# Three scatter accumulators in place of four, and a last round of ten grouped quads, in a message-passing layer on one Trainium2 core

## The chip, the cores and the metric

The kernel runs on one core of a Trainium2 chip. The core has five engines with a queue of instructions each, which run in order: TensorE (PE) multiplies matrices, VectorE (DVE) works on whole tiles, ScalarE (ACT) evaluates functions and copies, GpSimd (POOL) here mostly issues scatters, and SyncE (SP) issues loads and stores. Engines wait for one another by semaphores. The metric is the time of one execution on the device, in microseconds (us).

## The reference

The layer has 6250 nodes with 128 features and 200,000 edges. Each edge has a source node `src`, which receives, a node `dst`, from which it takes features, 20 attributes and a weight. The edges are sorted by `dst`; `src` is random.

```
h   = relu(layernorm(x)) @ W_in                       # 6250 x 128
W   = (softplus(f @ W_f1 + b_f1) - log 2) @ W_f2 + b_f2   # 200000 x 128
m   = h[dst] * W * weight                             # 200000 x 128
agg = segment_sum(m, src)                             # 6250 x 128
out = x + (softplus(agg @ W_o1 + b_o1) - log 2) @ W_o2 + b_o2
```

## The kernel before, in words

Edges are taken in chunks of 128, one to a partition: 1563 chunks, or 391 **quads** of four chunks (512 edges). One loop runs over items 0 to 398; each item does a stage of several neighbouring quads, so that all engines have work: the filter of quad i+1 (`s1_pe`, `s1_exp`, `s1_ln`), gather and product of quad i-1 (`s2_pe_x`, `s2_pe_w`, `s2_copy`, `s2_m`, lines 505 to 536), the last stages of quads i-2 to i-4. The order within an item is written out by hand at the loop's end (lines 1225 ff.). Everything else is hung into it by `at(item, point, function)`: points L (loads on SP), D0 to D2, DM and DR (DVE), A0 to A2 (ACT), PE1 and PE2 (PE), and S, the end of the item, for scatters. The kernel is scheduled by hand; each engine takes its instructions in that order.

`dst` is sorted, so a quad gathers from a short window of rows by a one-hot product. `src` is random, so the sum over edges is the hard part. A quad is summed in one of three ways:

- **plain** quads (31 of them: the first 12, and 19 at the end). `s3_pe` adds up rows of the same node within a chunk by a product with an equality matrix, `s3_copy` moves the result into a tile `s` (four buffers), `s3_ji` makes the indices `ji`, and `s3_scatter` adds 128 rows of 512 bytes to an accumulator in DRAM, one scatter a chunk, in item q+4.
- **listed** quads (192). The product is written into `s` at once and scattered in item q+2. Rows of a node that stands twice in a chunk go to a list area behind the accumulator. Windows of 16 listed quads each get their list ready ahead (`l_eq` to `l_take`) and are finished by `l_load`, which reads the list rows of every accumulator, `l_sum`, which adds them, and one more scatter.
- **grouped** quads (168; from quad 8 on, at steps of 2, 2, 2 and 3). `rank_group` and what follows it (lines 603 to 672) work out, for eight quads at a time, a slot for each edge by its node's group; `perm_oh` and `permute` move the rows to their slots (four blocks of 128) by one-hot products, `perm_out` copies them into `mst`. After a **round** of eight grouped quads four **units** follow (`unit_oh`, `unit_pe`, `unit_evac`): each adds one block of all the round's quads into `accT`, a transposed accumulator in SBUF. The units of the last round stand at items 389, 391, 393 and 395. Rows that find no slot are gathered for two quads at a time (`over_pe` to `over_int`) and scattered once (`over_scatter`, tiles `os` and `oji`).

All scatters are indirect DMAs that POOL issues from line 597, in the order of the program. `acc_of` gives the accumulator by the running count of scatters: accumulator 0 alone for the first two, two in turn up to the eighth, three in turn up to the 140th, four in turn up to the 923rd (`RET`, all but the last 64), and then accumulators 1 to 3. Two scatters to one accumulator don't overlap: the later one waits until the earlier one has landed. The accumulators are cleared by DMAs (`zero_piece`, line 168, and `zero_list`, line 173) during the first items.

As nothing goes to accumulator 0 after the 923rd scatter, items 376 to 397 read it early: `r0_load` (line 1084), four transposes in `r0_tp` (line 1091) and an addition to `accT` in `r0_add` (line 1097), for each of 13 groups of 512 nodes.

Behind the loop a few flags are worked out on DVE (lines 1285 to 1290); all engines read them, and there is a repair path that doesn't run with these inputs. Then the **tail** reads accumulators 1, 2 and 3 (`t_load`, line 1378), adds them up, transposes, adds `accT` and computes the output layer, for 13 groups of nodes. `over_int` (line 769) makes the scatter's indices on ACT in the item after the sum, at its end (point A2), from what DVE made in the same item.

Of the kernel before, what the change touches and what calls it, by code (L numbers as in the profile page):

```python
# [7 lines left out]
F32 = mybir.dt.float32  # L8
# [12 lines left out]
P = 128  # L21
# [5 lines left out]
SLOTS = GRP * CAP + OVC  # L27
MP0 = 8
MPGAPS = (2, 2, 2, 3)
MPEND = 0  # L30
RND = 8
EXTRA = 0
RKQ = 8
UOFF = (2, 6)
SW = 16
# [8 lines left out]
WSEG = 256  # L44
HB = 64
NR = 3 * WIN
NACC = 4
FPARTS = ((0, 3), (3, 2), (5, 1))
CQ = 16
EARLY_N = 256  # L50
# [4 lines left out]
def tile_gnn(ctx: ExitStack, tc: tile.TileContext, x, fB, cT, srcT, srcr, dstr, win_, wf1, wf2, bias, bo1c, wo1,  # L55
# [20 lines left out]
    GN = NP // GRP  # L76
    ZR = 10 if ACC_R % 10 == 0 else 1
    ZL = 3
    K1_END, K2_END, K3_END = 2, 8, 140
    Z2, Z3 = [0,0,1,1,2,2,3,3,4,4], [5+2*j for j in range(10)]  # L80
    mpq = sorted_quads(NQ)
    mpi = {q: n for n, q in enumerate(mpq)}
    units = unit_its(mpq)
# [4 lines left out]
    CE = min(128, EP // P) if spread else EP // P  # L88
    CB = min(4 * NS + 64, EP // P) if spread else 0
    lend = splain[LE - 1] if LE else 0  # L90
    scat = [0] * (NQ + 60)
    for q in splain:
        scat[q + (2 if LB <= plain[q] < LE else 4)] += min(4, NCH - 4 * q)
    NW = (LE - LB) // SW
    LR = P * NW
    wend = [splain[LB + SW * (w + 1) - 1] for w in range(NW)]
    for w in range(NW):
        scat[wend[w] + 16] += 1
    for q in mpq[1::2] + mpq[-1:] * (len(mpq) % 2):
        scat[q + 10] += 1  # L100
    RET = max(120, sum(scat) - 64)
    ret_at = min(i for i in range(len(scat)) if sum(scat[:i + 1]) >= RET)

    cp = ctx.enter_context(tc.tile_pool(name="cp", bufs=1))
    dp = ctx.enter_context(tc.tile_pool(name="dp", bufs=1, space=DRAM))
# [475 lines left out]
    def acc_of(k):  # L581
        if k < K1_END:
            return 0
        if k < K2_END:
            return k % 2
        if k < K3_END:
            return k % 3
        if k < RET:
            return k % 4
        return 1 + k % 3  # L590

    sc_n = [0]

# [9 lines left out]
    def rank_group(r):  # L603
        qs = mpq[RKQ * r:RKQ * r + RKQ]
        nc4 = 4 * len(qs)
        srcf = wk.tile([P, 4 * RKQ], F32, tag="srcf", name="srcf", bufs=1)
        o = 4 * (NS + RKQ * r)
        nc.vector.tensor_copy(srcf[:, :nc4], srcT_sb[:, o:o + nc4])
        srcf = srcf[:, :nc4]
        n = [P, nc4, GRP - 1]  # L610
        nc.vector.tensor_tensor(ge[:, :nc4, 1:GRP], srcf.unsqueeze(2).to_broadcast(n),
                                thr.unsqueeze(1).to_broadcast(n), op=ALU.is_ge)
        G = wk.tile([P, 4 * RKQ, GRP], BF16, tag="G", name="G", bufs=1)
        nc.vector.tensor_tensor(G[:, :nc4], ge[:, :nc4, :GRP], ge[:, :nc4, 1:], op=ALU.subtract)
        cnt = wk.tile([P, 4 * RKQ], F32, tag="cnt", name="cnt", bufs=1)
        nc.vector.tensor_reduce(cnt[:, :nc4], ge[:, :nc4, 1:GRP], axis=AX.X, op=ALU.add)
        loc = wk.tile([P, 4 * RKQ], F32, tag="loc", name="loc", bufs=1)
        nc.vector.scalar_tensor_tensor(loc[:, :nc4], cnt[:, :nc4], float(-GN), srcf, op0=ALU.mult, op1=ALU.add)
        ext = wk.tile([P, 4 * RKQ, 3], BF16, tag="ext", name="ext")
        nc.vector.memset(ext[:, :, 0], 0.0)  # L620
        nc.vector.tensor_scalar(ext[:, :nc4, 1], loc[:, :nc4], float(-(GN // 2)), None, op0=ALU.add)
        nc.vector.tensor_copy(ext[:, :nc4, 2], cnt[:, :nc4])
        rk[r] = {"G": G[:, :nc4], "cnt": cnt[:, :nc4], "ext": ext, "n": nc4, "qs": qs}

    def before_me(ps_t, src, w):
        n = src.shape[1]
# [223 lines left out]
    with tc.manual_schedule():  # L850
# [145 lines left out]
            at(2 * k + 3 if spread else 0, "D2", half_piece, k)  # L996
        for j in range(ZR):
            at(Z2[j] if spread else 0, "L", zero_piece, nc.sync, 2, j)
        for j in range(ZR):
            at(Z3[j] if spread else 0, "L", zero_piece, nc.sync, 3, j)  # L1000
        for g in range(1, NG):
            if not spread:
                xt_load(g)
# [74 lines left out]
        def large_all():  # L1078
            nc.vector.tensor_scalar(zcol[:, 3:4], late["lps"][:, 0:1], 0.0, None, op0=ALU.is_gt)

        def r0_load(g):
            o, T = tgroups[g]
            t_ = ld.tile([P, 4, P], F32, tag="fb", name="r0t", bufs=2)
            nc.sync.dma_start(wide(t_[:, :T], T), rows(accs[0], o, T))
            pst["r", g] = t_

        def r0_tp(g):
            T = tgroups[g][1]
            tp = ps.tile([P, 4, P], F32, tag="B", name="rtp", bufs=4)
            for t in range(T):  # L1090
                nc.tensor.transpose(tp[:, t, :], pst["r", g][:, t, :], idt)
            pst["p", g] = tp

        def r0_add(g):
            o, T = tgroups[g]
            v = nodes(accT, o, T)
            nc.vector.tensor_tensor(v, tiles(pst["p", g], T), v, op=ALU.add)

        def x_bias(t):
            n = min(4, NPT - t)  # L1100
            v = x_sb[:, t:t + n]
# [20 lines left out]
        for t in range(0, NPT, 4):  # L1122
            i = mid + 8 * (t // 4) if spread else 0
            at(min(i + 9, NQ + 1), "D2", x_bias, t)
        r0_at = 0
        for g in range(len(tgroups)):
            i = clear(max(r0_at + 1, ret_at + 5), units)
            r0_at = i
            at(i - 2, "L", r0_load, g)
            at(i, "PE2", r0_tp, g)  # L1130
            at(i + 1, "D0", r0_add, g)
        for r in range(-(-len(mpq) // RKQ)):
            i = mpq[RKQ * r]
            i = max(i, 6)
            at(i - 6, "D2", rank_group, r)
            at(i - 5, "PE2", rank_count, r)
            at(i - 4, "D0", rank_own, r)
            k = mpq[RKQ * r] if i == 6 else i - 2
            at(k, "PE2", rank_over, r)
            at(k + 1, "D0", rank_slot, r)  # L1140
# [3 lines left out]
        for w in range((LE - LB) // SW):  # L1144
            for g in range(4):
                n = LB + SW * (w - 1) + 4 * g
                i = splain[n] + 2 if w else 6 + 2 * g
                while w and (i - MP0) % sum(MPGAPS) not in UOFF:
                    i -= 1
                for k in range(2):  # L1150
                    kk = (LB + SW * w + 4 * g) // 2 + k
                    at(max(0, i + k - 2), "L", sb_load, kk)
                    at(i + k, "DM", l_eq, kk)
                i = clear(i + 2, units)
                at(i, "PE2", l_count, (LB + SW * w) // 4 + g)
                at(i + 1, "D0", l_dup, w, g)
            i += 1
            at(i, "D0", l_scan, w)
            i = clear(i, units)
            at(i, "PE2", l_before, w)  # L1160
            at(i + 1, "D0", l_index, w)
            assert i + 1 <= splain[LB + SW * w] + 1
            at(i + 2, "D2", l_id, w)
            i = clear(i + 3, units)
            at(i, "PE2", l_place, w)
            at(i + 1, "D0", l_take, w)
            i = clear(wend[w] + 12, units)
            at(i, "L", l_start, w)
            at(i, "A0", l_dg, w)
            at(i, "PE2", over_row, ("L", w))  # L1170
            at(i + 1, "D0", l_same, w)
            k = clear(i + 1, units)
            at(k - 1, "L", l_load, w)
            at(k, "PE2", l_sum, w)
            at(k + 1, "A0", l_copy, w)
            at(k + 1, "DM", l_ji, w)
            at(k + 1, "A2", over_int, ("L", w))
            at(k + 2, "S", over_scatter, ("L", w))
        if LE:
            for k in range(NACC):  # L1180
                for j in range(ZL):
                    at((0, 3, 6, 9)[k] + j + 1, "L", zero_list, k, j)
        for q in mpq:
            at(q + 1, "D2", perm_oh, q)
            at(q + 2, "DR", part_rem, q, 1)
# [11 lines left out]
            if mpi[q] % 2 or q == mpq[-1]:  # L1197
# [9 lines left out]
                at(k, "PE2", over_sum, q)  # L1207
                at(k + 1, "A0", over_copy, q)
                at(k + 1, "DM", over_ji, q)
                at(k + 1, "A2", over_int, q)  # L1210
                at(k + 2, "S", over_scatter, q)
        last = mpq[-1]
        for r in range(len(mpq) // RND):
            for s, k in enumerate(unit_slots(mpq, r)):
# [2 lines left out]
                at(k, "PE2", unit_pe, r, s)  # L1217
                at(k + 1, "D1", unit_evac, r, s)

        banked = (prep_tp, prep_mm, rank_count, rank_over, permute, over_pe, over_row, over_sum, late_bias, r0_tp,  # L1220
                  l_count, l_sum, l_before, l_place)
        full = {-1: False}
        r0_end = r0_at
        s1_pe(0)
        for i in range(max(NQ + 7, last + 16, r0_end + 2, lend + 24)):
            if i % 2 == 0 and i // 2 + 2 <= (NQ - 1) // 2:
                load_sc(i // 2 + 2)
            run(i, "L")
# [64 lines left out]
    with tc.For_i(0, redo, 1):  # L1293
        anew = nc.values_load(flagi[:, 1:2], min_val=0, max_val=1, skip_runtime_bounds_check_because="0 or 1")
        with tc.For_i(0, anew, 1):
            nc.vector.memset(accT, 0.0)
            for k in range(1, NACC):
                for j in range(ZR):
                    zero_piece(nc.sync, k, j)
        trips = nc.values_load(flagi[:, 0:1], min_val=0, max_val=NCH,  # L1300
# [70 lines left out]
    with tc.manual_schedule():  # L1371
# [8 lines left out]

        def t_sum1(g):
            T = tgroups[g][1]
            a2 = tl[g][2]
            nc.gpsimd.tensor_tensor(a2[:, :T], a2[:, :T], tl[g][3][:, :T], op=ALU.add)

        def t_sum2(g):
            T = tgroups[g][1]
            a1 = tl[g][1]
            eng = nc.vector if g % 2 else nc.gpsimd
            eng.tensor_tensor(a1[:, :T], a1[:, :T], tl[g][2][:, :T], op=ALU.add)  # L1390

        def t_tp(g):
            tp = pt.tile([P, 4, P], F32, tag="tp", name="tp")
            for t in range(tgroups[g][1]):
                nc.tensor.transpose(tp[:, t, :], tl[g][1][:, t, :], idt)
            tl[g]["tp"] = tp

        def t_cp(g):
# [52 lines left out]
            del tl[g]  # L1451

        for g in range(min(TAIL_AHEAD, TG)):
            for k in (1, 2, 3):
                t_load(g, k)
        for j in range(-1, TG + 4):
            if TAIL_AHEAD <= j + TAIL_AHEAD < TG:
                for k in (1, 2, 3):
                    t_load(j + TAIL_AHEAD, k)
            if j + 1 < TG:  # L1460
                t_sum1(j + 1)
# [162 lines left out]
```

## Time and profile before

| | |
|---|---|
| median of 3 runs | 2063.21 us (2060.39 to 2073.85) |
| the profiled execution's own time | 2063.64 us, span 2061.9 us |
| mean granted TensorE clock | 0.952 |
| PE busy | 1820.4 us (88%) |
| DVE busy | 1650.9 us (80%) |
| POOL busy | 1652.4 us (80%) |
| ACT busy | 1470.8 us (71%) |
| DMA | 272.41 MB, mean 132 GB/s |

The span runs from the first to the last instruction of the program. Busy time counts an engine's own instructions, not its waits, and not the sequencer's pieces between two instructions. A row of a group has a line, an engine, an operation, the tiles (out<-in), the count, and then busy time, the mean length of one in ns, and the idle time just before, with what ended most of it. A row of waits has who waited, for whom, the total, the number of times and the longest, in us. In a row of the timeline stand start, length, engine, line, operation, tiles and count. A row of a stretch has its bounds and length, busy time and count (for one engine or for each), the granted clock, the share of the DMA engines and GB/s.

### The profile page before, as it was taken

The page shows a single profiled execution, that of the slowest core. Times are in us where ns is not written, and L with a number is a line of the kernel's source. Part 1 is how long each engine was busy: PE and PEld are TensorE (multiplying, and loading weights), DVE is VectorE, ACT ScalarE, POOL GpSimd, SP SyncE. Part 2 cuts the span into 40 slices and gives each one's busy share as a digit, 9 for nine tenths or more (in the row PEclk, how much of TensorE's full clock was granted, in tenths as well). Part 3 has the DMA queues.
Part 4 walks back from the last instruction along what each step waited for, and adds up shares of the span by engine and source line. Part 5 has one row for each costly group of instructions (what it writes and reads, how often), then busy time and mean ns, then how long its engine had stood idle before and what let it go on. Part 6 is the DMA issues. An engine that isn't in the chain of part 4 may idle for free.

```text
span 2061.9 us, 54889 instructions
## 1 busy us (share of the span) xinstructions
PE 1820.4 (88%) x19121; PEld 1188.1 (58%) x19121; DVE 1650.9 (80%) x4449; ACT 1470.8 (71%) x3999; POOL 1652.4 (80%) x1040
## 2 busy tenths in 40 slices
PE   2578998899999999899989999999799899999966
PEld 1455555556655665565656566566565556666734
DVE  3577897798987988888888989888788687787745
ACT  2458776777777787777778787787677677788714
POOL 3578887888888888878788888888888888888884
PEclk9789999999999999999999999999999999999987
DMA  6887766667676776667666666766666666667647
GB/s 240 242 202 141 129 123 123 111 111 144 118 136 120 128 136 111 130 115 131 129 121 125 121 126 117 126 117 132 113 116 114 125 105 118 108 119 141 128 44 250
DMA packets 359675, 272.41 MB, mean 132 GB/s; under 512 B 97727, under 2 KB 319850, under 8 KB 359394
## 3 DMA queue, kind: packets, MB, share of 16 engines
q0 software_dynamic: 143728, 71.30, 34.4%
q1 hardware_dynamic: 215378, 197.50, 32.8%
q8 instruction: 151, 2.47, 0.5%
q14 instruction: 130, 1.06, 0.2%
q10 hardware_dynamic: 288, 0.07, 0.0%
HBM read 154.45 MB, written 114.24 MB: 130 GB/s over the span
## 4 chain that ended last, share of the span: by engine, by line
PE 46%; DVE 20%; ACT 10%; DMA 7%; issue 6%; POOL 5%; SPq 4%; DVEq 0%; ACTq 0%; POOLq 0%
PE pq L702 15%; PE W L520 10%; PE un L795 8%; POOL acc L597 5%; ACT xc L525 3%; PE po L715 2%; DVE accT L806 2%; DVE pt L691 2%; PE z L328 2%; ACT mst L708 2%; DVE eql L384 2%; PE xg L512 2%; DMA acc<-s,lji 2%; DVE pm L677 2%; ACT a L333 2%
## 5 line engine op out<-in xcount | busy, mean ns | idle before, releaser
L597 POOL DMA_INDIRECT acc<-s,lji x768 | 1254.4, 1633 | 250.4 <-issue 185.5
L702 PE MATMUL pq<-pt,pm 128*128 128x387 bf16 x2688 | 545.6, 346 | 43.2 <-ACT pt L697 10.6
L525 ACT ACTIVATE xc<-xg,cb 128x128 f32<-128x128 f32 x1564 | 448.0, 377 | 80.5 <-PE xg L512 73.4
L520 PE MATMUL W<-w,a 128*128 128x128 f32 x3128 | 467.7, 294 | 0.0
L520 PEld LDWEIGHTS W<-w,a 128*128 128x128 f32 x3128 | 392.2, 197 | 42.9 <-issue 4.5
L708 ACT CAST mst<-pq 128x387 bf16<-128x387 f32 x672 | 305.4, 481 | 149.7 <-PE pq L702 108.7
L702 PEld LDWEIGHTS <-pm 128*128 128x128 bf16 x2688 | 261.1, 100 | 235.6 <-issue 60.9
L795 PE MATMUL un<-so,mst 32*128 32x392 bf16 x8064 | 372.5, 327 | 11.9 <-ACT s L555 5.8
L795 PEld LDWEIGHTS <-mst 32*128 32x128 bf16 x8064 | 226.1, 93 | 152.0 <-issue 45.3
L338 ACT ACTIVATE a<-a,con 128x512 f32<-128x512 f32 x391 | 282.3, 722 | 12.7
L597 POOL DMA_INDIRECT acc<-s,ji x123 | 198.4, 1613 | 80.1 <-issue 26.7
L333 ACT ACTIVATE a<-z 128x512 f32<-128x512 f32 x391 | 238.0, 609 | 30.5 <-PE z L328 20.1
L691 DVE TENSOR_TENSOR pt<-pt 128x512 f32<-128x512 f32 x336 | 231.6, 689 | 5.8
L535 DVE TENSOR_TENSOR pt<-W,xc 128x512 f32<-128x512 f32 x168 | 115.5, 687 | 132.4 <-PE po L715 62.9
L677 DVE TENSOR_SCALAR pm<-iot,pos 128x576 bf16<-128x576 f16 x672 | 219.8, 388 | 0.0
L535 DVE TENSOR_TENSOR s<-W,xc 128x512 f32<-128x512 f32 x192 | 131.8, 686 | 75.7 <-ACT xc L525 44.6
L780 DVE TENSOR_SCALAR so<-iot,mst 128x392 bf16<-128x392 f16 x672 | 181.2, 333 | 9.7 <-PE un L795 9.2
L597 POOL DMA_INDIRECT acc<-os,oji x96 | 158.1, 1647 | 30.4 <-issue 18.3
L806 DVE TENSOR_TENSOR accT<-un,accT 128x392 f32<-128x392 f32 x320 | 158.4, 557 | 28.6 <-PE un L795 18.9
L512 PE MATMUL xg<-wn,oh 63*128 63x128 bf16 x1564 | 158.9, 224 | 25.0 <-DVE oh L345 13.8
L328 PE MATMUL z<-ft,ws 123*128 123x512 bf16 x391 | 151.7, 388 | 15.5 <-POOL b2rep L942 9.3
L509 PE MATMUL W<-b2rep,onesb 64*128 64x512 bf16 x391 | 155.6, 398 | 0.2 <-issue 0.2
(210 smaller groups left out, 1968.1 us busy)
## 6 DMA issues: line engine op xcount, KB each, us to landing
rb<-reld SPq DMA_DIRECT2D x391, 64.0 KB
fsd<-f SPq DMA_DIRECT2D x49, 480.0 KB
ft<-fsd SPq DMA_DIRECT2D x195, 120.0 KB
sb<-src SPq DMA_DIRECT2D x169, 128.0 KB
fb<-in_fB_dram SPq DMA_DIRECT2D x49, 320.0 KB
ft<-fsd SPq DMA_DIRECT2D x195, 80.0 KB
wn<-tab SPq DMA_DIRECT2D x782, 15.8 KB
acc<-s,lji POOLq DMA_INDIRECT x768
```

The source lines that it names most:

```text
L333: nc.scalar.activation(a, st[q]["z"], AF.Exp)
L338: nc.scalar.activation(a, a, AF.Ln, bias=half, scale=0.5)
L512: nc.tensor.matmul(xg[:, c, :], st[q]["oh"][a:a + NR, c * P:(c + 1) * P], wn[a:a + NR, c // 2, :], start=True, stop=True)
L520: nc.tensor.matmul(W[:, c, :], st[q]["a"][:, c * P:(c + 1) * P], w2, start=False, stop=(c == 3))
L525: nc.scalar.mul(xc[:, c, :], st[q]["xg"][:, c, :], late["c", q // CQ][:, 4 * (q % CQ) + c:4 * (q % CQ) + c + 1])
L535: nc.vector.tensor_tensor(m[:, :, :P], st[q]["W"], st[q]["xc"], op=ALU.mult)
L597: nc.gpsimd.indirect_dma_start(out=accs[k][:rows, :], out_offset=bass.IndirectOffsetOnAxis(ap=ji, axis=0), in_=s, in_offset=None, compute_ ...
L677: nc.vector.tensor_scalar(pm[:, c], iot[:, :SLOTS], rk[r]["pos"][:, 4 * j + c:4 * j + c + 1], None, op0=ALU.is_equal)
L691: nc.vector.tensor_tensor(pt[:, :, k * P:(k + 1) * P], a, high(a), op=ALU.subtract)
L702: nc.tensor.matmul(t[:, :PW], mp[q]["pm"][:, c, s * P:(s + 1) * P], high(mp[q]["pt"][:, c:c + 1, :PW])[:, 0], start=(c == 0), stop=(c == 3))
L708: nc.scalar.copy(mp[q]["ms", s][:, :PW], mp[q].pop(("q", s))[:, :PW])
L795: nc.tensor.matmul(ts[g][:, :GN], mp[q]["ms", s][v, k * P:(k + 1) * P], mp[q]["oh"][v], start=(q == qs[0] and k == 0), stop=(q == qs[-1] a ...
```

## The change

Five edits come together.

1. Three accumulators (`NACC = 3`), taken in turn from the ninth scatter to the end. The fourth one's clearing (ten `zero_piece` and three `zero_list` DMAs) and its part in `l_load` and `l_sum` go, and so does the early reading of accumulator 0 (`r0_load`, `r0_tp`, `r0_add`). The tail reads accumulators 0, 1 and 2.
2. `MPEND = 1` and `EXTRA = 2`: there are 170 grouped quads in place of 168. Quads 386 and 388, plain before, are grouped, so that 29 plain quads are left. The last round has ten quads, and its units stand at items 394, 396, 398 and 400. The loop has 404 items in place of 399.
3. `mst` of the first block and `so`, the one-hot tiles of the units, get ten buffers in place of eight.
4. `over_int` moves from point A2 of item k+1 to point A0 of item k+2; the scatter stays at the end of item k+2.
5. `rank_group` is cut in two: the counts and what is made of them (`rank_local`) follow an item later.

```diff
-MPEND = 0
+MPEND = 1
 RND = 8
-EXTRA = 0
+EXTRA = 2
...
-NACC = 4
+NACC = 3
...
         if k < K2_END:
             return k % 2
-        if k < K3_END:
-            return k % 3
-        if k < RET:
-            return k % 4
-        return 1 + k % 3
+        return k % 3
...
         nc.vector.tensor_tensor(G[:, :nc4], ge[:, :nc4, :GRP], ge[:, :nc4, 1:], op=ALU.subtract)
+        rk[r] = {"G": G[:, :nc4], "n": nc4, "qs": qs, "srcf": srcf}
+
+    def rank_local(r):
+        nc4, srcf = rk[r]["n"], rk[r]["srcf"]
         cnt = wk.tile([P, 4 * RKQ], F32, tag="cnt", name="cnt", bufs=1)
...
-        for j in range(ZR):
-            at(Z3[j] if spread else 0, "L", zero_piece, nc.sync, 3, j)
...
-        r0_at = 0
-        for g in range(len(tgroups)):
-            i = clear(max(r0_at + 1, ret_at + 5), units)
-            r0_at = i
-            at(i - 2, "L", r0_load, g)
-            at(i, "PE2", r0_tp, g)
-            at(i + 1, "D0", r0_add, g)
...
             at(i - 6, "D2", rank_group, r)
+            at(i - 5, "D2", rank_local, r)
...
-            at(k + 1, "A2", over_int, ("L", w))
+            at(k + 2, "A0", over_int, ("L", w))
             at(k + 2, "S", over_scatter, ("L", w))
...
-                    at((0, 3, 6, 9)[k] + j + 1, "L", zero_list, k, j)
+                    at((0, 3, 6)[k] + j + 1, "L", zero_list, k, j)
...
-                at(k + 1, "A2", over_int, q)
+                at(k + 2, "A0", over_int, q)
                 at(k + 2, "S", over_scatter, q)
...
-        for i in range(max(NQ + 7, last + 16, r0_end + 2, lend + 24)):
+        for i in range(max(NQ + 7, last + 16, lend + 24)):
...
-            for k in (1, 2, 3):
+            for k in range(NACC):
                 t_load(g, k)
```

More of the change, by code (lines that the diff above doesn't have):

```diff
@@ L78, in tile_gnn @@
     ZL = 3
-    K1_END, K2_END, K3_END = 2, 8, 140
-    Z2, Z3 = [0,0,1,1,2,2,3,3,4,4], [5+2*j for j in range(10)]
+    K1_END, K2_END = 2, 8
+    Z2 = [0, 0, 1, 1, 2, 2, 3, 3, 4, 4]
     mpq = sorted_quads(NQ)
@@ L90, in tile_gnn @@
     lend = splain[LE - 1] if LE else 0
-    scat = [0] * (NQ + 60)
-    for q in splain:
-        scat[q + (2 if LB <= plain[q] < LE else 4)] += min(4, NCH - 4 * q)
     NW = (LE - LB) // SW
@@ L96, in tile_gnn @@
     wend = [splain[LB + SW * (w + 1) - 1] for w in range(NW)]
[L97 to L102, printed above, removed]
     cp = ctx.enter_context(tc.tile_pool(name="cp", bufs=1))
@@ L622, in rank_group @@
         nc.vector.tensor_copy(ext[:, :nc4, 2], cnt[:, :nc4])
-        rk[r] = {"G": G[:, :nc4], "cnt": cnt[:, :nc4], "ext": ext, "n": nc4, "qs": qs}
+        rk[r]["cnt"], rk[r]["ext"] = cnt[:, :nc4], ext
     def before_me(ps_t, src, w):
@@ L1079, in large_all @@
             nc.vector.tensor_scalar(zcol[:, 3:4], late["lps"][:, 0:1], 0.0, None, op0=ALU.is_gt)
[L1081 to L1097, printed above, removed]
         def x_bias(t):
@@ L1218, in tile_gnn @@
                 at(k + 1, "D1", unit_evac, r, s)
-        banked = (prep_tp, prep_mm, rank_count, rank_over, permute, over_pe, over_row, over_sum, late_bias, r0_tp,
+        banked = (prep_tp, prep_mm, rank_count, rank_over, permute, over_pe, over_row, over_sum, late_bias,
                   l_count, l_sum, l_before, l_place)
         full = {-1: False}
-        r0_end = r0_at
         s1_pe(0)
-        for i in range(max(NQ + 7, last + 16, r0_end + 2, lend + 24)):
+        for i in range(max(NQ + 7, last + 16, lend + 24)):
             if i % 2 == 0 and i // 2 + 2 <= (NQ - 1) // 2:
@@ L1296, in tile_gnn @@
             nc.vector.memset(accT, 0.0)
-            for k in range(1, NACC):
+            for k in range(NACC):
                 for j in range(ZR):
@@ L1382, in t_sum1 @@
             T = tgroups[g][1]
-            a2 = tl[g][2]
-            nc.gpsimd.tensor_tensor(a2[:, :T], a2[:, :T], tl[g][3][:, :T], op=ALU.add)
+            a1 = tl[g][1]
+            nc.gpsimd.tensor_tensor(a1[:, :T], a1[:, :T], tl[g][2][:, :T], op=ALU.add)
         def t_sum2(g):
             T = tgroups[g][1]
-            a1 = tl[g][1]
+            a0 = tl[g][0]
             eng = nc.vector if g % 2 else nc.gpsimd
-            eng.tensor_tensor(a1[:, :T], a1[:, :T], tl[g][2][:, :T], op=ALU.add)
+            eng.tensor_tensor(a0[:, :T], a0[:, :T], tl[g][1][:, :T], op=ALU.add)
         def t_tp(g):
@@ L1394, in t_tp @@
             for t in range(tgroups[g][1]):
-                nc.tensor.transpose(tp[:, t, :], tl[g][1][:, t, :], idt)
+                nc.tensor.transpose(tp[:, t, :], tl[g][0][:, t, :], idt)
             tl[g]["tp"] = tp
@@ L1453, in tile_gnn @@
         for g in range(min(TAIL_AHEAD, TG)):
-            for k in (1, 2, 3):
+            for k in range(NACC):
                 t_load(g, k)
@@ L1457, in tile_gnn @@
             if TAIL_AHEAD <= j + TAIL_AHEAD < TG:
-                for k in (1, 2, 3):
+                for k in range(NACC):
                     t_load(j + TAIL_AHEAD, k)
```

## The prediction

> **What bounds the kernel now.** I read the page's busy times first, then its costliest groups, then the scatters' groups by stretches of time, then the waits of GpSimd (POOL) in those stretches, and the end of the chain last.
>
> ```profile
> span 2061.9 us, 54889 instructions
> ...
> PE 1820.4 (88%) x19121; PEld 1188.1 (58%) x19121; DVE 1650.9 (80%) x4449; ACT 1470.8 (71%) x3999; POOL 1652.4 (80%) x1040
> ...
> PE 46%; DVE 20%; ACT 10%; DMA 7%; issue 6%; POOL 5%; SPq 4%; DVEq 0%; ACTq 0%; POOLq 0%
> ...
> L597 POOL DMA_INDIRECT acc<-s,lji x768 | 1254.4, 1633 | 250.4 <-issue 185.5
> ...
> L597 POOL DMA_INDIRECT acc<-s,ji x123 | 198.4, 1613 | 80.1 <-issue 26.7
> ...
> L597 POOL DMA_INDIRECT acc<-os,oji x96 | 158.1, 1647 | 30.4 <-issue 18.3
> ```
>
> TensorE (PE) is busiest and leads the chain, so it looks like the bound. But POOL has 768 + 123 + 96 = 987 scatters, and "busy" leaves out an idle piece ahead of each one. The rows by stretch have the time, the busy time and the count; the waits have the total, the times and the longest. The waits' first row is of 700 to 1200, the other two of 1200 to 1890.
>
> ```profile
> 60.00:190.00 130.00, 92.15 (x56) 0.83 0.82 201
> 190.00:350.00 160.00, 130.81 (x81) 0.96 0.67 121
> ...
> 700.00:1200.00 500.00, 413.31 (x253) 0.97 0.68 126
> 1200.00:1890.00 690.00, 581.37 (x357) 0.97 0.66 118
> 1890.00:2010.00 120.00, 97.94 (x63) 0.92 0.60 97
> ```
>
> ```profile
> POOL acc L597 <- DVE s L535: 11.8, 7, 3.3
> ...
> POOL acc L597 <- issue: 86.3, 283, 0.3
> POOL acc L597 <- DMA acc<-s,lji: 5.8, 19, 0.3
> ```
>
> From 1200 to 1890 no wait of these is over 0.3 us: 86.3 / 283 = 0.30 us is the fixed piece between two scatters. So POOL never lacks work there; a scatter costs 690 / 357 = 1.93 us, and 97.94 / 63 + 0.30 = 1.86 us in the end run. Before 1200 POOL was short of data seven times, 11.8 - 7 x 0.30 = 9.7 us in all. From 1200 on POOL alone sets the time. The stop of ScalarE (ACT) in that time fits:
>
> ```profile
> 1450.00:1500.00 50.00, 38.81 (x401) 25.00 (x393) 35.89 (x86) 30.18 (x81) 42.38 (x26) 0.90 0.57 98
> ...
> L769 ACT ACTIVATE oji<-ojd,con 128x1 int32<-128x1 f32 x96 | 29.5, 308 | 64.8 <-DMA acc<-os,oji 35.5 <-DVE ojd L765 21.9 <-issue 4.4
> ```
>
> PE falls to 38.81 of 50 us, POOL stays at 42.38: others wait for the scatters. The end shows it without PE in the picture (start, length to its landing, who):
>
> ```profile
> 2007.27 3.23 DMA acc<-os,oji
> ```
>
> ```profile
> 1996.72 1.98 DVE L806 TENSOR_TENSOR accT<-un,accT 128x392 f32<-128x392 f32 x4 [5.26 <-PE un L795]
> ...
> 1999.26 0.13 DVE L1289 TENSOR_SCALAR flagi<-flag 1x1 int32<-1x1 f32 x1
> ...
> 2011.37 20.22 SPq L1378 DMA_DIRECT2D ta_in<-acc  x30
> ```
>
> The compute is through at 1999.39, the last scatter starts at 2007.27, and the tail's first load follows 4.1 us behind that start. The tail then takes 2061.9 - 2011.4 = 50.5 us. It reads three accumulators before and after, with the same sums, so I leave it at that.
>
> **The change, part by part.**
>
> *Seven scatters fewer.* Two plain quads with four scatters each become grouped, and one overflow scatter is added: 987 becomes 980. They fall in the end run, back to back: 7 x 1.86 = **-13 us** on POOL.
>
> *Three accumulators in place of four* from the 141st scatter to the 923rd, 783 of them. A scatter waits until the previous one on its accumulator has landed; that one started 4 x 1.86 = 7.4 us earlier or more, and now 3 x 1.86 = 5.6 us. The kernel already runs with three in two stretches. Two rows of 190 to 350, two of 1890 to 2010, then a landing on the chain:
>
> ```profile
> POOL acc L597 <- DMA acc<-s,lji: 3.0, 5, 0.9
> ...
> POOL acc L597 <- DMA acc<-os,oji: 1.0, 1, 1.0
> ...
> POOL acc L597 <- DMA acc<-s,ji: 2.5, 7, 0.7
> POOL acc L597 <- DMA acc<-os,oji: 1.5, 1, 1.5
> ```
>
> ```profile
> 1940.13 3.74 DMA acc<-s,ji
> ```
>
> Less 0.30 for each, that is 2.2 us over 81 scatters (0.027 each) and 1.6 us over 63 (0.025; without its one long wait 0.006). The two landings on the chain, 3.74 and 3.23 us, fit into 5.6, so only the late ones cost. Ends: 0.006 x 783 = 5 us and 0.027 x 783 = 21 us. I take 15, nearer to the stretch from 190, whose DMA share of 0.67 is that of the middle (0.66 to 0.68). Behind the waiting scatter stand all later scatters and, through their buffers, the products. By count 8 of the 15 fall before 1200, where POOL's 9.7 us without data swallow them; **+7 us** stay.
>
> The Trainium skill, "DMA: Bandwidth & Descriptors", section "Anatomy of one DMA", gives a DMA issued by GpSimd about 2.0 us plus its bytes over 436 GB/s; for 64 KB that would be 2.15 us, an estimate by that page. No scatter would then ever wait on three accumulators and this term would be 0; the trace has 3.2 to 3.7 us and a few waits, so I don't follow it.
>
> *No fourth accumulator to clear.* Ten clearing DMAs and three for the list rows leave SyncE's (SP's) queue in the start-up:
>
> ```profile
> L168 SPq DMA_DIRECT2D acc<-accT x20: 360/430/614, 45.9 to 173.4; - x20
> ...
> 50.00:150.00 100.00, 65.71 (x451) 49.21 (x452) 68.19 (x170) 52.98 (x151) 62.42 (x37) 0.76 0.85 226
> ...
> POOL acc L597 <- DMA acc<-s,ji: 22.7, 16, 4.7
> ```
>
> Issue time: 13 x 0.43 = 5.6 us. The start is slow on all engines, the DMA engines are 0.85 busy, and POOL waits 22.7 - 16 x 0.30 = 18 us for landings from 60 to 190 (the last row). A gain from 0 to 10 us; I take **-4**, below the issue time, as half of these DMAs stand beside waits that stay.
>
> *The early reading of accumulator 0 goes*: 13 loads on SP, 49 transposes and 13 additions on VectorE (DVE) in items 376 to 397.
>
> ```profile
> L1091 PE MATMUL rtp<-idt,r0t 128*128 128x128 f32 x49 | 7.6, 276 | 0.9 <-DVE accT L806 0.5 <-ACT s L555 0.3
> ```
>
> The 7.6 us stand beside POOL's scatters: nothing, and a gain of 7.6 us where PE bounds. One load and one product fewer for each of twelve list windows lie beside POOL too: nothing.
>
> *Indices one item later.* ACT's 35.5 us for index buffers and 21.9 us for DVE shrink. Both are beside POOL: nothing. Before 1200 they may cut into its 9.7 us, which are spent already. The scatter stands at the end of the item in which ACT now makes its index, an item of some 2061.9 / 399 = 5.2 us; were that cover gone, POOL would wait up to 5 us an overflow where its queue is short.
>
> *Rank preparation in two pieces* issues the same DVE instructions an item apart, with a 22nd group of two quads: nothing, since DVE has room even in the densest stretch.
>
> ```profile
> 1890.00:1955.00 65.00, 64.93 (x637) 47.05 (x637) 50.53 (x126) 53.72 (x156) 52.98 (x34) 1.00 0.73 140
> ```
>
> *Ten quads in the last round, and the units five items later* (394, 396, 398, 400, not 389 to 395). This is the one part that can come out behind POOL, so I follow PE (busy for 64.93 of these 65 us) to the end:
>
> ```profile
> 1923.55 3.02 PE L702 MATMUL pq<-pt,pm 128*128 128x387 bf16 x16
> ...
> 1947.59 1.05 PE L547 MATMUL pp<-m,eq 128*128 128x129 f32 x8
> ...
> 1956.08 0.34 PE L795 MATMUL un<-so,mst 32*128 32x392 bf16 x2
> ...
> 1957.67 4.41 PE L795 MATMUL un<-so,mst 32*128 32x392 bf16 x94 [1.25 <-ACT s L555]
> ...
> 1964.98 0.39 PE L509 MATMUL W<-b2rep,onesb 64*128 64x512 bf16 x1
> ...
> 1972.23 7.19 PE L795 MATMUL un<-so,mst 32*128 32x392 bf16 x94 [4.50 <-ACT s L555]
> ...
> 1983.14 4.13 PE L795 MATMUL un<-so,mst 32*128 32x392 bf16 x93 [0.19 <-DVE accT L1097]
> ```
>
> Item 391 began at 1964.98. Out come the unit of item 389 (1956.1 to 1962.1, 6 us) and the transposes of ten of the 13 node groups (7.6 x 40 / 49 = 6 us); in goes the permutation of a quad for its plain product (3.02 - 1.05 = +2 us): 1955. From there two permutations, two plain products and the rest of items 391 and 392, some 8 us, lead to the first unit at 1963. A unit of 120 products takes 4.13 x 120 / 93 = 5.3 us, and about 2.2 us pass until DVE has emptied its banks (1.98 us above): 7.5 us a unit. The last is added by 1963 + 3 x 7.5 + 5.3 + 2.2 = 1993, flags by 1994. From flags to first load all is hidden in this trace; between 0 and the 4.1 us behind the last scatter, I take 2.5: 1997. POOL: 2007.3 + 4.1 - 13 + 7 - 4 = 2001. POOL still decides, by 4 us.
>
> **Sum**: -13 + 7 - 4 = -10. Span 2052; with the 1.7 us around it (2063.64 for a span of 2061.9) **2054 us**. The profiled execution is within 0.5 us of the median of 2063.21.
>
> **Rivals.**
>
> *A: three accumulators cost more (slower).* A landing later than 5.6 us stops all scatters behind it. For: the start-up, on two and three accumulators, lost 18 us in the 56 scatters of 60 to 190, 0.32 each. Against: its DMA share was 0.82 or more, the middle has 0.66. It decides from 0.034 a scatter on (783 x 0.034 = 27, less the 9.7, eats the 17 us gained); at 0.05 it is 39 - 9.7 - 17 = +12, 2076; at 0.065, +24, 2088.
>
> *B: the units end last.* With idle time between them PE may run slow: 94 products took 7.19 us after 4.50 us of idling. At that rate a unit is 9.2 + 2.2 us: last addition at 1963 + 4 x 11.4 = 2009, first load at 2012, no gain: 2064; with half of them slow 2056. Against: the gaps would be about 2 us. The Trainium skill, "TensorE: Matmul & The Clock Gate", section "Part 1: The HAM clock gate", has the clock halve after an idle window of about 3.4 us; the 7.19 us beside 4.13 agrees.
>
> *C: landings never matter and the start gains in full.* Then -13 - 10 on POOL; the units, six microseconds earlier than above, hold the tail at 1991: -20, 2043. For: both landings on the chain are under 4 us. The rule on DMAs quoted above would lead here.
>
> *D: the change takes scatters off an engine that doesn't bound.* If PE is the bound, it has two quads' permutations and four longer units more, 4 + 4.7 us, and 7.6 us of transposes less: 2065. For: PE leads the chain with 46%. Against: POOL's waits from 1200 on.
>
> **How the numbers follow.** Forecast 0.38 (2047 to 2062), A 0.30, B 0.12, C 0.15, D 0.05. One per cent of the median, what a measurement here can tell from no change, is 2043 to 2084. Of A 0.18 lies above; of C half, 0.08, lies below. That leaves 0.74 within. The range runs from 2040, C with its start a little better, to 2088, A at 0.065.
>
> **What would show it.** POOL with 980 scatters; its waits for landings from 350 to 1890 at 5 to 21 us above 0.30 each, not near 1; from 60 to 190 fewer than 22.7 us; the last scatter near 1997, the last addition of a unit near 1995, the first tail load near 2001. Scatter waits of 30 us or more, or a tail load that follows the flags and not the scatters, make me wrong.

## The result, and the profile after

The change makes the kernel a little slower: 2069.47 us median (2061.22 to 2082.31, 21 runs) against 2060.74 us (2054.55 to 2073.85, 21 runs), a ratio of 1.0035 with an interval of [1.0021, 1.005]. By the ratio that is +7 us where -10 us was forecast. The time lies in the range, and the sign is wrong. Three of the experiments beat both kernels; the best is the changed kernel with four accumulators, at 0.9913 [0.9888, 0.9938].

The first profile of the changed kernel is of its slowest execution (2082.31 us). Its page, lines as in the one before (scatters are now on line 584):

```profile
span 2080.5 us, 54963 instructions
...
PE 1834.9 (88%) x19181; PEld 1199.4 (58%) x19181; DVE 1652.7 (79%) x4473; ACT 1476.1 (71%) x4008; POOL 1652.3 (79%) x1033
```

A second profile of the same kernel (run `e9_after_again` below; span 2070.5 us) lies nearer to the median, so the readings are made on it. First the largest group of scatters of the kernel before, with more of its idle time than the page shows, then the changed kernel's groups of scatters and the line of the overflow indices:

```profile
L597 POOL DMA_INDIRECT acc<-s,lji x768 | 1254.4, 1633 | 250.4 <-issue 185.5 <-DMA acc<-s,lji 17.2 <-DVE s L535 13.3
...
L584 POOL DMA_INDIRECT acc<-s,lji x768 | 1260.3, 1641 | 265.0 <-issue 178.4 <-DMA acc<-s,lji 46.1 <-DVE s L526 5.0
...
L584 POOL DMA_INDIRECT acc<-s,ji x115 | 187.4, 1630 | 77.0 <-issue 25.7 <-ACT ji L569 21.4 <-DMA acc<-s,ji 19.3
L584 POOL DMA_INDIRECT acc<-os,oji x97 | 157.6, 1624 | 32.0 <-issue 15.1 <-ACT mst L699 5.1 <-DMA acc<-s,lji 2.9
...
L760 ACT ACTIVATE oji<-ojd,con 128x1 int32<-128x1 f32 x97 | 27.4, 283 | 72.4 <-DMA acc<-os,oji 59.3 <-DVE ojd L756 6.9 <-DVE accT L797 3.1
```

There are 768 + 115 + 97 = 980 scatters, as forecast. Their busy time and the idle time ahead of them come to 1605.3 + 374.0 = 1979.3 us; before it was 1610.9 + 360.9 = 1971.8 us. So POOL's queue is 7.5 us longer although it holds seven scatters fewer, and the last scatter starts 7.4 us later (2014.63, not 2007.27). The idle time rose by 13.1 us. Busy time fell by 5.6 us, less than seven scatters (7 x 1.63 = 11.4 us), so the others took some 6 us longer in all. The time "<-DMA acc<-s,lji", waits for landings, went from 17.2 to 46.1 us in the largest group.

The scatters can also be counted in the two timelines. The 141st is the first of the middle, where the kernel before takes four accumulators in turn; the 924th is the first behind it. The 141st and the 924th of the kernel before, then of the changed kernel:

```profile
357.10 1.64 POOL L597 DMA_INDIRECT acc<-s,lji  x1 [0.58 <-DVE pt L535]
...
1887.37 1.55 POOL L597 DMA_INDIRECT acc<-s,ji  x1 [0.31 <-issue]
```

```profile
353.06 1.55 POOL L584 DMA_INDIRECT acc<-s,lji  x1 [0.30 <-issue]
...
1906.99 1.55 POOL L584 DMA_INDIRECT acc<-s,ji  x1 [0.30 <-issue]
```

The middle begins 4.0 us earlier and takes 1553.9 us in place of 1530.3, so 23.7 us more. From the 924th to the last scatter it is 107.6 us in place of 119.9, so 12.3 us less, and from there to the end of the span 1.2 us more. The sum is +8.6 us, the difference of the two spans (2070.5 and 2061.9).

POOL's waits by stretches show where in the middle. First the kernel before from 350 to 1200 (from 1200 on its row stands in the prediction: 19 waits of 0.30 us each), then the changed kernel from 350 to 1200 and, behind the dots, from 1200 to 1880:

```profile
POOL acc L597 <- DVE s L535: 12.4, 9, 3.3
POOL acc L597 <- DMA acc<-s,lji: 8.7, 27, 0.7
```

```profile
POOL acc L584 <- DMA acc<-s,lji: 26.0, 39, 2.1
POOL acc L584 <- DVE s L526: 3.8, 9, 1.1
...
POOL acc L584 <- DMA acc<-s,lji: 16.4, 29, 2.1
```

Less the fixed 0.30 us for each, landings cost 0.6 us before in the first stretch, and 26.0 - 11.7 = 14.3 us and 16.4 - 8.7 = 7.7 us after: 22 us. The middle's 23.7 us have other parts too. In the first stretch POOL's time without data (`DVE s`), less its fixed pieces, fell from 9.7 to 1.1 us. The 783 scatters themselves took 5 us longer in all (1284.8 us, not 1279.8), and the rest stands in small waits for other engines.

The start is as forecast. The stretch from 60 to 190 and its waits (before: 0.82 busy, 201 GB/s, and 22.7 us in 16 waits):

```profile
60.00:190.00 130.00, 93.99 (x57) 0.82 0.77 172
```

```profile
POOL acc L584 <- DMA acc<-s,ji: 16.6, 8, 6.0
```

The DMA engines are 0.77 busy, and the waits less 0.30 us each fell from 17.9 to 14.2 us.

The end, from the timelines of PE, POOL, DVE and SP, put together:

```profile
1985.00 8.45 PE L786 MATMUL un<-so,mst 32*128 32x392 bf16 x120 [4.27 <-ACT s L546]
...
2012.94 5.13 PE L786 MATMUL un<-so,mst 32*128 32x392 bf16 x117 [0.15 <-DVE accT L797]
...
2014.63 1.54 POOL L584 DMA_INDIRECT acc<-os,oji  x1 [0.31 <-DVE so L771]
...
2017.96 1.98 DVE L797 TENSOR_TENSOR accT<-un,accT 128x392 f32<-128x392 f32 x4 [3.58 <-PE un L786]
...
2020.66 4.65 SPq L1342 DMA_DIRECT2D ta_in<-acc  x9
```

The last scatter alone would have let the tail start 4.1 us after its own start, at 2018.7. The last unit's addition ends at 2019.9 and the tail starts at 2020.7: units and scatters end within some two microseconds of each other, the units last.

### The profile page after: what moved, and what is told of

Read it like the earlier page. It is cut to its first block, busy times and chain, and to the rows that moved or that the text cites. A ratio compares the mean times of both kernels' runs of the same rounds, so it can differ in the third digit from the quotient of the medians.

```text
span 2080.5 us, 54963 instructions
## 1 busy us (share of the span) xinstructions
PE 1834.9 (88%) x19181; PEld 1199.4 (58%) x19181; DVE 1652.7 (79%) x4473; ACT 1476.1 (71%) x4008; POOL 1652.3 (79%) x1033
## 5 line engine op out<-in xcount | busy, mean ns | idle before, releaser
L511 PE MATMUL W<-w,a 128*128 128x128 f32 x3128 | 472.8, 296 | 0.0
L511 PEld LDWEIGHTS W<-w,a 128*128 128x128 f32 x3128 | 396.6, 199 | 43.2 <-issue 5.3
L699 ACT CAST mst<-pq 128x387 bf16<-128x387 f32 x680 | 309.6, 483 | 147.3 <-PE pq L693 106.7
L693 PEld LDWEIGHTS <-pm 128*128 128x128 bf16 x2720 | 265.9, 101 | 222.5 <-issue 50.0
L786 PE MATMUL un<-so,mst 32*128 32x392 bf16 x8160 | 379.2, 327 | 12.1 <-ACT s L546 3.3
L786 PEld LDWEIGHTS <-mst 32*128 32x128 bf16 x8160 | 234.0, 93 | 151.2 <-issue 46.6
L329 ACT ACTIVATE a<-a,con 128x512 f32<-128x512 f32 x391 | 283.3, 725 | 12.7
L584 POOL DMA_INDIRECT acc<-s,ji x115 | 187.3, 1629 | 73.4 <-issue 27.7
```

The lines of the kernel that those rows point to most:

```text
L329: nc.scalar.activation(a, a, AF.Ln, bias=half, scale=0.5)
L511: nc.tensor.matmul(W[:, c, :], st[q]["a"][:, c * P:(c + 1) * P], w2, start=False, stop=(c == 3))
L584: nc.gpsimd.indirect_dma_start(out=accs[k][:rows, :], out_offset=bass.IndirectOffsetOnAxis(ap=ji, axis=0), in_=s, in_offset=None, compute_ ...
L693: nc.tensor.matmul(t[:, :PW], mp[q]["pm"][:, c, s * P:(s + 1) * P], high(mp[q]["pt"][:, c:c + 1, :PW])[:, 0], start=(c == 0), stop=(c == 3))
L699: nc.scalar.copy(mp[q]["ms", s][:, :PW], mp[q].pop(("q", s))[:, :PW])
L786: nc.tensor.matmul(ts[g][:, :GN], mp[q]["ms", s][v, k * P:(k + 1) * P], mp[q]["oh"][v], start=(q == qs[0] and k == 0), stop=(q == qs[-1] a ...
```

## The experiments

Each run is told against the kernel before, run beside it on the same chip. Two theories were set against each other first. **Theory 1**: POOL's queue of scatters sets the time, and the loss is the waits for landings that three accumulators bring. **Theory 2**: the loss comes from the end, or from ACT's stops.

**Three accumulators in the middle, all else as before.**

```diff
         if k < RET:
-            return k % 4
+            return k % 3
```

> The kernel before, with one size changed: the scatters from the 141st to RET (the last 64 excepted) go to three accumulators in turn; the fourth is still cleared and read, and all else is as before. Theory 1 (the queue of scatters sets the time, and each wait for a landing is added to it): waits of POOL for landings rise from about 1 us to about 20 us between 350 and 1890, and the time rises by 12 to 22 us (ratio 1.006 to 1.011), as the part of them that falls before 1200 can hide behind POOL's 10 us without data. Theory 2 (the loss of the changed kernel comes from its end, units after the last scatter, or from ScalarE's stops): no change, within 4 us.

Measured: ratio 1.0103 [1.0069, 1.0137], 2077.29 us against 2055.87 us: **21 us slower**, from a change of one number. Theory 2 is out as the main cause. The waits, from 350 to 1200 and then from 1200 to 1880:

```profile
POOL acc L597 <- DMA acc<-s,lji: 14.8, 28, 1.5
...
POOL acc L597 <- DMA acc<-s,lji: 12.7, 24, 1.1
```

In this one execution they are 14.8 - 8.4 + 12.7 - 7.2 = 12 us over their fixed pieces, where about 20 us were expected. That is less than the 22 us of the changed kernel and less than the 21 us by which the median moved; the profiled execution's 2072.76 us is at the low end of its runs (2070.04 to 2086.34). Counted by scatters, its middle took 1538.1 us. In the run with the later indices further below, on the same chip and as fast as the kernel before, the middle took 1521.0 us: 17.1 us of the 17.6 us between these two spans lie there, so the named waits are not all of what the accumulators cost.

One such wait, from the timeline and from the chain:

```profile
1294.59 1.64 POOL L597 DMA_INDIRECT acc<-s,lji  x1 [0.31 <-DVE s L535]
...
1300.93 1.54 POOL L597 DMA_INDIRECT acc<-s,lji  x1 [1.01 <-DMA acc<-s,lji]
```

```profile
1294.59 5.89 DMA acc<-s,lji
```

The scatter at 1300.93 is the third after the one at 1294.59, so it has the same accumulator, and that one landed only after 5.89 us.

**Two accumulators in the middle**: the dose raised.

```diff
         if k < RET:
-            return k % 4
+            return k % 2
```

> The kernel before with two accumulators in turn from the 141st scatter to RET, four still cleared and read: the dose is raised. Theory 1: a scatter must then wait for the one before the last, which lands 3.2 to 3.7 us after its start, and starts another 0.9 us later; (3.6 + 0.9) / 2 = 2.25 us a scatter in place of 1.93, so 0.3 us x 783 = some 250 us slower (200 to 300), and POOL's waits name a landing at nearly every second scatter. If landings don't matter, no change.

Measured (two executions): 1.1386 [1.135, 1.1422], 2347.9 us against 2062.97 us, so 285 us slower. Scatters by stretch, the kernel before and then this one, and the waits of this one from 1200 to 1880:

```profile
1200.00:1880.00 680.00, 572.89 (x352) 0.97 0.66 119
```

```profile
1200.00:1880.00 680.00, 480.62 (x299) 0.89 0.57 102
```

```profile
POOL acc L597 <- DMA acc<-s,lji: 94.2, 82, 3.4
POOL acc L597 <- issue: 50.7, 151, 0.9
```

680 / 352 = 1.93 us a scatter became 680 / 299 = 2.27 us, where 2.25 was worked out from the landing. The expectation of a named wait at nearly every second scatter was too high, 82 and some others of 299. The landing is what a scatter waits for, and from four to three to two accumulators its cost goes from nothing over 21 us to 285 us.

**Everything but the accumulators.** The changed kernel with `NACC = 4`, the fourth accumulator's clearing, `acc_of` and the early reading as before.

```diff
+MPEND = 1
+EXTRA = 2
...
+            at(i - 5, "D2", rank_local, r)
...
+            at(k + 2, "A0", over_int, ("L", w))
...
+                at(k + 2, "A0", over_int, q)
```

> The changed kernel with its accumulators as before: four of them, accumulator 0 read early, three read in the tail. Last round of ten, indices an item later and rank preparation in two pieces stay. Theory 1: seven scatters fewer take 13 us off the queue, so 8 to 13 us faster (ratio 0.994 to 0.996). Theory 2 (the units of the last round come out behind the scatters): the gain is eaten, 0 to +4 us, and the tail's first load follows the flags by 2 to 3 us instead of the last scatter by 4 us.

Measured: 0.9913 [0.9888, 0.9938], 2039.62 us: **18 us faster**, more than expected. From this version to the changed kernel the accumulators cost 1.0035 / 0.9913 = 1.012, about 25 us. Its end (POOL, DVE, SP):

```profile
1984.42 1.54 POOL L597 DMA_INDIRECT acc<-os,oji  x1 [0.30 <-DMA acc<-s,ji]
...
1987.90 1.98 DVE L810 TENSOR_TENSOR accT<-un,accT 128x392 f32<-128x392 f32 x4 [3.73 <-PE un L799]
...
1990.59 19.74 SPq L1383 DMA_DIRECT2D ta_in<-acc  x30
```

The scatters would have let the tail start at 1988.5; it starts 0.7 us after the last unit's addition, at 1990.6. The units take back 2 us of the gain here too, not all of it.

**The last round of ten alone.**

```diff
-MPEND = 0
+MPEND = 1
...
-EXTRA = 0
+EXTRA = 2
```

> The kernel before with the last round of ten grouped quads alone. Theory 1: as the run with all but the accumulators, 8 to 13 us faster, because the other two edits lie beside the scatters. Theory 2: no gain, the units end last. If this one gains and the run with all but the accumulators doesn't, the later indices or the cut rank preparation cost.

Measured: 0.9948 [0.9927, 0.9969], 2048.83 us, so **11 us faster**. The seven scatters count in full but for the two microseconds at the end: from the 924th to the last it takes 107.6 us here too.

**Later indices and cut rank preparation alone.**

```diff
+            at(i - 5, "D2", rank_local, r)
...
-            at(k + 1, "A2", over_int, ("L", w))
+            at(k + 2, "A0", over_int, ("L", w))
...
-                at(k + 1, "A2", over_int, q)
+                at(k + 2, "A0", over_int, q)
```

> The kernel before with the indices an item later and the rank preparation in two pieces alone. Theory 1: nothing, within 3 us; ScalarE's 21.9 us of waiting for VectorE at the index line go, and no scatter starts later. Theory 2 (an index that is made an item later holds ScalarE at its next item's start, ahead of the products): 4 to 10 us slower, with longer stops of ScalarE for index buffers than 35.5 us.

Measured: 0.9995 [0.9976, 1.0014], no change. The index line of this run (its line number is shifted):

```profile
L773 ACT ACTIVATE oji<-ojd,con 128x1 int32<-128x1 f32 x96 | 26.8, 282 | 41.4 <-DMA acc<-os,oji 32.8 <-DVE accT L810 3.1 <-DVE ojd L769 2.9
```

ACT's wait for DVE fell from 21.9 to 2.9 us, and nothing came of it. Beside the last round the two edits may bring something: 0.9913 with them, 0.9948 without. The intervals overlap, so that stays open.

**The accumulators' edit alone.** The changed kernel with the constants, `over_int` and `rank_group` as before.

```diff
-NACC = 4
+NACC = 3
...
-        if k < RET:
-            return k % 4
-        return 1 + k % 3
+        return k % 3
...
-            at(i - 2, "L", r0_load, g)
```

> The kernel before with the accumulators' edit alone: three of them, no clearing of a fourth, no early reading of accumulator 0, all three read at the end. Theory 1: the waits of the run with three in the middle (+21 us there) less some 5 us of start-up: +13 to +20 us, ratio 1.006 to 1.010; 987 scatters, the last one some 15 us later than before. If the edits added up, this ratio times that of the run with all but the accumulators (0.9913) would give the changed kernel's 1.0035, so 1.012; a lower one says that the waits cost more where the queue has less time to spare.

Measured: 1.0084 [1.0057, 1.011], 2082.92 us against 2062.97 us, 17 us slower. If the edits add up, this ratio times 0.9913 is the changed kernel's: 1.0084 x 0.9913 = 0.9996. The 1.0015 of the next run lies within what the intervals allow; the 1.0035 of the result is at their edge, so a part of the accumulators' cost may hang on the other edits.

**The changed kernel again.**

> The changed kernel as it is, for a profile nearer to its median than the first one (2082 us, its slowest run) and beside the others on one chip. Theory 1: POOL's waits for landings between 350 and 1890 come to about 20 us above 0.30 us each, from 60 to 190 they are below the 22.7 us of before; the time is 1.002 to 1.005 of the kernel before.

Measured: 1.0015 [0.9994, 1.0036], just under the expected 1.002 to 1.005, and not clear of no change. Its profile is read above: the waits came as expected, 22 us from 350 to 1880 and 16.6 us from 60 to 190.

**Four index buffers in the changed kernel.** ACT stops for a free index buffer for 59.3 us in the second profile of the changed kernel (77.0 us in the first), for 35.5 us before. That is a rival cause (theory 3).

```diff
-        ji = sp_.tile([P, 1], I32, tag="oji", name="oji", bufs=2)
+        ji = sp_.tile([P, 1], I32, tag="oji", name="oji", bufs=4)
```

> The changed kernel with four buffers in place of two for the overflow scatters' indices (tile oji). ScalarE's stops for a free index buffer (some 75 us in the changed kernel's profile, 35.5 us before) go or shrink to a few us. Theory 1 (POOL's queue of scatters sets the time, the stops are only its back-pressure): no change against the changed kernel, within 5 us, so ratio 1.001 to 1.006 against the kernel before. Theory 3 (the longer stops are what made the change slower): 10 to 30 us faster than the changed kernel, ratio 0.990 to 0.999.

Measured: 1.0021 [0.9996, 1.0045], beside 1.0015 for the changed kernel on the same chip.

```profile
L760 ACT ACTIVATE oji<-ojd,con 128x1 int32<-128x1 f32 x97 | 26.9, 281 | 9.8 <-DVE ojd L756 7.7 <-issue 2.1
```

The stops are gone altogether, and the time is the same. They were back-pressure of the scatters, not a cause. Theory 3 falls.

**Three accumulators in the first half, or in the second half.** The prediction let the waits before 1200 hide. These two runs ask that question.

```diff
-    K1_END, K2_END, K3_END = 2, 8, 140
+    K1_END, K2_END, K3_END = 2, 8, 566
```

> The kernel before with three accumulators in turn up to the 566th scatter (about 1190 us) in place of the 140th; four after that. The prediction's step: the waits there, about 11 us, hide behind POOL's time without data, so 0 to 3 us slower. Rival (that time without data stays, as the landings' waits fall at other places): 8 to 15 us slower, ratio 1.004 to 1.007.

```diff
         if k < RET:
-            return k % 4
+            return k % 3 if k >= 566 else k % 4
```

> The kernel before with four accumulators up to the 566th scatter and three from there to RET. Both readings: nothing hides the waits after 1190 us, 357 scatters at 0.027 to 0.03 us: 9 to 13 us slower, ratio 1.004 to 1.007. If this one costs 20 us and the first half nothing, the prediction's hiding holds and only the size was off.

Measured: first half 1.0039 [1.0019, 1.0058], +8 us; second half 1.0059 [1.0037, 1.0082], +12 us. Together that is 20 us, where the middle as a whole gave 21. The first half isn't free. The waits of the first-half run from 350 to 1200 and (behind the dots) from 1200 to 1880, and those of the second-half run from 350 to 1200 and (behind the dots) from 1200 to 1880:

```profile
POOL acc L597 <- DMA acc<-s,lji: 18.5, 39, 1.3
...
POOL acc L597 <- DMA acc<-s,lji: 2.7, 9, 0.3
```

```profile
POOL acc L597 <- DVE s L535: 9.7, 9, 3.3
POOL acc L597 <- DMA acc<-s,lji: 9.5, 26, 1.1
...
POOL acc L597 <- DMA acc<-s,lji: 16.6, 26, 1.7
```

Landing waits sit where three accumulators are: 18.5 - 11.7 = 6.8 us and then nothing in the first run; in the second 1.7 us up to 1200 and 16.6 - 7.8 = 8.8 us after. POOL's time without data (`DVE s`) is 9.7 - 2.7 = 7 us with four accumulators there, and the first run has only 1.2 us in 4 waits, which is the fixed piece. So that idle time did give way to the waits, and the first half still cost 8 us. Counted by scatters, the 141st to the 567th take 843.4 us in the first-half run and 832.3 us in the second-half run; 5.5 us of these 11 are the scatters' own time (700.3 us, not 694.8), and why they take longer is not shown.

**Clearing the fourth accumulator later**, in the version with everything but the accumulators, to have the start's gain as well.

```diff
-    Z2, Z3 = [0,0,1,1,2,2,3,3,4,4], [5+2*j for j in range(10)]
+    Z2, Z3 = [0,0,1,1,2,2,3,3,4,4], [17+j for j in range(10)]
...
-                    at((0, 3, 6, 9)[k] + j + 1, "L", zero_list, k, j)
+                    at((0, 3, 6, 23)[k] + j + 1, "L", zero_list, k, j)
```

> Four accumulators with the last round of ten, later indices and the cut rank preparation (the run with all but the accumulators), and the fourth accumulator's clearing moved from items 5 to 23 to items 17 to 26. Theory 1: the 141st scatter starts some 2 to 5 us earlier, as it does in the changed kernel (351 to 355 us, not 357), because the clears leave the crowded start; ratio 0.988 to 0.992 against the kernel before. Rival: the clears only collide later, no change from 0.9913.

Measured: 0.9929 [0.9908, 0.9951], 2041.96 us, no better than 0.9913. The gain of the start couldn't be had this way. In its trace the 141st scatter does start earlier, at 352.3 us against 354.2 us in the version that it was made from, but the 924th starts at 1877.8 us against 1877.3 us: what the start gained was gone by then. This is one execution of each, and whether the clears collide with something later was not settled.

## Why the prediction was wrong, step by step

- **What bounds the kernel**: right. Seven scatters fewer gave 11 us, ACT's stops of 59.3 us could be removed without any effect, and a change of one number in the scatters' order moved the time by 21 us. Rival D (PE is the bound) is out.
- **Seven scatters fewer, -13 us**: right within 2 us (-11 us alone, with the units' 2 us taken off).
- **Three accumulators, +7 us**: this is the step that failed, twice. Its mechanism was right. The first failure is the size: I took 15 us, and the run with three in the middle measured 21 us [14 to 28, by its interval]. The 0.027 us a scatter of the stretch from 190 gives 21 as well, but that it agrees so well is partly luck: it comes from six waits in one execution. The same stretch runs on three accumulators in every kernel here. Its waits for landings in the runs with the later indices and with three in the middle:

```profile
POOL acc L597 <- DMA acc<-s,lji: 1.6, 3, 0.9
```

```profile
POOL acc L597 <- DMA acc<-s,lji: 5.2, 6, 1.6
```

Less 0.30 us each that is 0.7 and 3.4 us over 81 scatters, or 7 and 33 us over 783. The second failure is the cover: I let 8 us hide behind POOL's 9.7 us without data before 1200, and the run with three in the first half cost 8 us there. The idle time went, but the half did not stay as long as it was. Nor was the cover sure: it differs between executions with the same first half, 9.7 us in the profile of the kernel before, 7 us in the run with three in the second half, and 5.6 - 1.8 = 3.8 us in the run with the last round alone:

```profile
POOL acc L597 <- DVE s L535: 5.6, 6, 2.8
```

- **No fourth accumulator to clear, -4 us**: borne out by the traces, not shown by the times. The 141st scatter starts at 350.7 to 354.7 us in the four traces that leave the clearing out, and at 354.2 to 359.6 us in the eight that have it at its old place. The waits for landings from 60 to 190, which I named as the sign, are too uneven for it: they fell by 3.7 us in the pair above, but the changed kernel with four index buffers has 21.7 - 13 x 0.30 = 17.8 us, as much as before. The edit alone cost 17 us where three in the middle cost 21 us, and these two intervals overlap.
- **The later indices, the cut rank preparation, the early reading, at nothing**: right for the first two (0.9995). The early reading and the shorter list sums were never undone alone.
- **The last round at the end**: POOL was to decide by 4 us; the units came last, by 2 us. I had the first unit begin at 1963 us, and it began at 1985.0 us. PE stood 4.27 us for ACT, whose copy of a plain quad's rows waited for a landing, and the unit then took 8.45 us, not 5.3. ACT's row, and PE's busy time and granted clock (the column behind the count) in the first and the last unit:

```profile
1984.57 0.65 ACT L546 COPY s<-pp 128x258 f32<-128x258 f32 x2 [5.61 <-DMA acc<-s,ji]
```

```profile
1985.00:1993.50 8.50, 8.36 (x120) 0.68 0.44 41
...
2012.90:2018.10 5.20, 5.13 (x117) 1.00 0.44 43
```

So the units hang on POOL's queue too. I had added the landings' waits to POOL's end alone and left the units where PE's own time put them. The 2.5 us that I took from flags to first load turned out as 0.7 us behind the last addition. Rival B was right in kind, and small.

- **The sum**: with +21 in place of +7, and +2 for the units, -13 + 21 - 4 + 2 = +6 us; measured +7 us. Counted by scatters above, the same terms are -12.3, +23.7, -4.0 and +1.2 us. Rival A, to which I gave 0.30, is what happened, at 0.027 us a scatter. I had it decide from 0.034 on, because the 9.7 us stood in that sum too.

Three accumulators cost 21 us, and two, where the scatter before on the same accumulator started 2 x 1.93 = 3.9 us earlier, cost 285 us. The rule on DMAs quoted in the prediction (the Trainium skill, "DMA: Bandwidth & Descriptors", section "Anatomy of one DMA") would have had no scatter wait on either, as its estimate of 2.15 us is below that and below the 3 x 1.93 = 5.8 us of three; here the measurement decides against it.

The first unit's 120 products took 8.45 us at a granted clock of 0.68 behind 4.27 us of idle time, and 117 products took 5.13 us at 1.00 later. The rule on the clock gate quoted in the prediction (the Trainium skill, "TensorE: Matmul & The Clock Gate", section "Part 1: The HAM clock gate") agrees with that.

## What to carry to other kernels

When an engine's queue is full from end to end, small waits in it add up to time, however rare they are: 0.03 us a scatter were 21 us here. Where the trace already holds a stretch that runs the new way, its rate is the right thing to multiply out, but a handful of waits is a small sample, and other executions of the same stretch would have given 7 or 33 us. Idle time seen elsewhere in one execution is poor cover for a cost: the next execution may not have it, and here the half that had it cost 8 us all the same. When a queue gets longer, move everything that waits for its buffers along with it, and not its last instruction alone. And a long stop of another engine that waits for the full queue is a symptom: taking 59 us of it away changed nothing.

## What the runs showed of the hardware that was not expected

One accumulator more or less decides between free and costly in a narrow band. At 1.93 us a scatter, four in turn show 0.6 us of waits for landings over their fixed pieces from 350 to 1880; three in the middle cost 21 us over 783 scatters, and two cost 285 us. The two landings that the prediction shows took 3.2 and 3.7 us, well under the 5.6 us that three allow, but they do not speak for the middle: the scatter shown above landed after 5.89 us. It is the late landings that count. From 350 to 1880 the second profile of the changed kernel names 68 waits for landings of listed quads' scatters, the longest of 2.1 us. What makes a landing late was not looked into.
